# Loading fields in pairs and late weights by GpSimd's queue over 14 of 16 DMA engines

## The chip, the cores and the metric

The kernel runs on one core of one Trainium2 chip. The metric is the device time of one execution in microseconds (us). A core has five engines that matter here: TensorE (PE, with its weight loads shown apart as PEld), VectorE (DVE), ScalarE (ACT), GpSimd (POOL) and SyncE (SP, which here only issues transfers, 93 in before). Their transfers run on 16 DMA engines: the page of before books the packets of all queues on them, 99.6% of their time in sum. Times are quoted as medians. Profiled executions have a "span", which is about 1.8 us shorter than the time.

## The reference

For 1024 samples with 32 fields of 128 numbers, every pair of fields i < j (496 pairs) has its own 128 x 128 matrix:

```python
v_i = inputs[:, I_IDX, :]
v_j = inputs[:, J_IDX, :]
transformed = jnp.einsum('bpd,ped->bpe', v_i, W)
return transformed * v_j
```

The result is 496 x 128 x 1024 float32, 260 MB.

## The kernel before

The pairs run from the last field down to the first, so that fields are needed one after the other: all pairs with the same i form a *field group*. Except for the first 15 pairs, each matmul is done as three, with x and W split into high and low parts to keep accuracy. For the weights, ScalarE makes the high part (`wh` in the profiles), GpSimd the low part (`wl`) and a difference (`wd`):

```python
    def split_w(c, u):          # c is a chunk of 2 pairs
        ...
        nc.scalar.mul(h, raw, 1.0 - 2.0**-13)
        nc.gpsimd.tensor_tensor(l, raw, h.bitcast(F32), ALU.subtract)
        nc.gpsimd.tensor_scalar(d, h.bitcast(F32), EPS, 1.0, ALU.mult, ALU.mult)
        nc.gpsimd.tensor_tensor(d, l.bitcast(F32), d.bitcast(F32), ALU.subtract)
```

At each field group GpSimd also has to split the next field (`split_x`: twice `xl`, twice a scaling, and for later fields twice `xd`).

The main loop, for each half pair `u` (cut):

```python
            if u % 2 == 0 and j == i + 1 and 0 < i - 2 - XLEAD:
                load_x(i - 2 - XLEAD)          # 512 KB by SyncE, 7 field groups ahead
            first(u)                           # two matmuls, ScalarE scales the sum
            if u % 2 == 1 and q in w_at:
                load_w(w_at[q])                # 8 pairs of weights, 512 KB by SyncE
        ...
            second(u - LAG)                    # third matmul, VectorE multiplies by x_j
        while stores and stores[0][0] <= u - LAG:
            nc.scalar.dma_start(*stores.pop(0)[1:])   # 4 pairs, 2 MB, by ScalarE's queue
```

## Time and profile before

| | before |
|---|---|
| time, median of 3 | 755.34 us (755.04 to 755.51) |
| span; mean granted PE clock (1 is full speed) | 753.2 us; 0.994 |
| DMA | 310 MB in 33,038 packets, 412 GB/s |
| landing gap of a store: last engine after the middle one (the 9th of 16), median, 30 to 80 us / 140 to 440 us / 440 to 720 us | 1.5 / 4.2 to 4.6 / 4.2 to 4.7 us |

The last row comes from the trace's records of semaphores: each of the 16 engines reports its share of each store. VectorE's pauses end with the last of them: in 69 of the 72 pauses of over 0.7 us in before, it goes on 0.12 us after the 16th report of a transfer.

### The profile page before, as it was taken

The page shows a single profiled execution, that of the slowest core. Times are in us where ns is not written, and L with a number is a line of the kernel's source. Part 1 is how long each engine was busy: PE and PEld are TensorE (multiplying, and loading weights), DVE is VectorE, ACT ScalarE, POOL GpSimd, SP SyncE. Part 2 cuts the span into 40 slices and gives each one's busy share as a digit, 9 for nine tenths or more (in the row PEclk, how much of TensorE's full clock was granted, in tenths as well). Part 3 has the DMA queues.
Part 4 walks back from the last instruction along what each step waited for, and adds up shares of the span by engine and source line. Part 5 has one row for each costly group of instructions (what it writes and reads, how often), then busy time and mean ns, then how long its engine had stood idle before and what let it go on. Part 6 is the DMA issues. An engine that isn't in the chain of part 4 may idle for free.

```text
span 753.2 us, 10948 instructions
## 1 busy us (share of the span) xinstructions
PE 706.5 (94%) x2946; PEld 546.0 (72%) x2946; DVE 624.1 (83%) x1012; ACT 627.1 (83%) x1256; POOL 595.5 (79%) x863
## 2 busy tenths in 40 slices
PE   7989999999999999999999999999999999999993
PEld 3567776777777777777777778777777777777782
DVE  4989888888887878888878897988888889888894
ACT  1389888889988898888888889898989898988892
POOL 1788998888988987978879797888887879796660
PEclk9999999999999999999999999999999999999997
DMA  9999999999999999999999999999999999999997
GB/s 353 428 427 423 430 427 424 423 417 433 399 425 406 411 420 413 415 405 401 425 401 422 412 401 422 400 432 405 417 419 421 399 432 401 425 406 413 425 397 312
DMA packets 33038, 310.04 MB, mean 412 GB/s; under 512 B 3665, under 2 KB 3793, under 8 KB 17361
## 3 DMA queue, kind: packets, MB, share of 16 engines
q10 hardware_dynamic: 19584, 261.10, 82.5%
q1 hardware_dynamic: 13392, 48.24, 16.8%
q8 instruction: 24, 0.39, 0.2%
q14 instruction: 38, 0.30, 0.1%
HBM read 49.28 MB, written 260.05 MB: 411 GB/s over the span
## 4 chain that ended last, share of the span: by engine, by line
DMA 43%; PE 32%; DVE 13%; POOL 6%; ACT 2%; issue 2%; DVEq 0%; ACTq 0%; POOLq 0%
DMA out_dram<-ot 42%; PE po L172 19%; DVE ot L187 12%; PE po L181 9%; PE po L169 4%; ACT po L173 2%; POOL xd L122 2%; POOL wl L102 1%; POOL xl L117 1%; POOL wd L104 1%; ACT wh L101 1%; POOL xl L118 1%; POOL wd L103 0%; DVE xd L217 0%; DMA x<-in_xt_dram 0%
## 5 line engine op out<-in xcount | busy, mean ns | idle before, releaser
L187 DVE TENSOR_TENSOR ot<-po,x 128x512 f32<-128x512 f32 x992 | 610.1, 682 | 118.5 <-DMA out_dram<-ot 50.7
L173 ACT ACTIVATE po<-po 128x512 f32<-128x512 f32 x962 | 543.4, 583 | 94.3 <-PE po L172 41.0
L172 PE MATMUL po<-xh,wh 128*128 128x512 f32 x962 | 382.8, 398 | 21.4 <-DVE ot L187 20.5
L172 PE MATMUL po<-xl,wl 128*128 128x512 f32 x962 | 376.6, 392 | 4.8 <-POOL wl L102 4.8
L181 PE MATMUL po<-xd,wd 128*128 128x512 f32 x962 | 375.2, 390 | 4.0 <-DVE xd L217 3.4
L172 PEld LDWEIGHTS po<-xh,wh 128*128 128x128 f32 x962 | 180.4, 188 | 88.8 <-DVE ot L187 50.8
L102 POOL TENSOR_TENSOR wl<-w,wh 128x256 fp32r<-128x256 f32 x241 | 178.3, 740 | 73.3 <-ACT wh L101 71.8
L181 PEld LDWEIGHTS po<-xd,wd 128*128 128x128 f32 x962 | 180.6, 188 | 44.0 <-ACT po L173 4.7
L172 PEld LDWEIGHTS po<-xl,wl 128*128 128x128 f32 x962 | 180.7, 188 | 42.2 <-POOL wl L102 8.8
L104 POOL TENSOR_TENSOR wd<-wl,wd 128x256 fp32r<-128x256 f32 x241 | 180.5, 749 | 20.1
L103 POOL TENSOR_SCALAR wd<-wh 128x256 fp32r<-128x256 f32 x241 | 101.3, 420 | 20.3
L101 ACT ACTIVATE wh<-w 128x256 fp32r<-128x256 f32 x241 | 99.5, 413 | 5.1 <-DVE ot L187 3.3
L117 POOL TENSOR_TENSOR xl<-x,xh 128x512 fp32r<-128x512 f32 x52 | 67.2, 1292 | 18.1 <-ACT xh L116 17.7
L122 POOL TENSOR_TENSOR xd<-xh,xl 128x512 fp32r<-128x512 f32 x32 | 41.4, 1294 | 2.7
L116 ACT ACTIVATE xh<-x 128x512 fp32r<-128x512 f32 x52 | 32.5, 629 | 11.3 <-DMA x<-in_xt_dram 11.2
L118 POOL TENSOR_SCALAR xl<-xl 128x512 fp32r<-128x512 f32 x52 | 33.7, 649 | 4.6
L169 PE MATMUL po<-x,w 128*128 128x512 f32 x60 | 27.8, 623 | 4.4 <-DMA x<-in_xt_dram 4.3
L169 PEld LDWEIGHTS po<-x,w 128*128 128x128 f32 x60 | 11.6, 198 | 19.8 <-issue 12.3
L217 DVE TENSOR_TENSOR xd<-xh,xl 128x512 fp32r<-128x512 f32 x20 | 17.2, 859 | 0.0
L116 ACT ACT_TABLE_LOAD x1 | 1.3, 1283 | 2.6 <-issue 2.6
L233 POOL MEMSET const-float32-0.0<- 128x1 f32 x1 | 0.1, 98 | 0.2 <-issue 0.2
L233 POOL MEMSET const-bfloat16-1.0<- 128x1 bf16 x1 | 0.1, 101 | 0.0
(2 smaller groups left out, 0.2 us busy)
## 6 DMA issues: line engine op xcount, KB each, us to landing
out_dram<-ot ACTq DMA_DIRECT2D x122, 2048.0 KB, 12.5
w<-in_wt_dram SPq DMA_DIRECT2D x61, 512.0 KB, 10.3
x<-in_xt_dram SPq DMA_DIRECT2D x30, 512.0 KB, 16.0
out_dram<-ot ACTq DMA_DIRECT2D x6, 512.0 KB, 9.2
x<-in_xt_dram ACTq DMA_DIRECT2D x4, 256.0 KB, 5.9
out_dram<-ot ACTq DMA_DIRECT2D x4, 256.0 KB, 8.2
w<-in_wt_dram SPq DMA_DIRECT2D x1, 448.0 KB, 4.7
w<-in_wt_dram SPq DMA_DIRECT2D x1, 64.0 KB, 2.9
```

The costliest lines, as they stand in the source:

```text
L101: nc.scalar.mul(h, raw, 1.0 - 2.0**-13)
L102: nc.gpsimd.tensor_tensor(l, raw, h.bitcast(F32), ALU.subtract)
L103: nc.gpsimd.tensor_scalar(d, h.bitcast(F32), EPS, 1.0, ALU.mult, ALU.mult)
L104: nc.gpsimd.tensor_tensor(d, l.bitcast(F32), d.bitcast(F32), ALU.subtract)
L117: nc.gpsimd.tensor_tensor(l, x_sb[f][:, s], h.bitcast(F32), ALU.subtract)
L118: nc.gpsimd.tensor_scalar(l, l.bitcast(F32), 1.0 / EPS, 1.0, ALU.mult, ALU.mult)
L122: nc.gpsimd.tensor_tensor(d, h.bitcast(F32), l.bitcast(F32), ALU.subtract)
L169: nc.tensor.matmul(po[u], w_raw[q // WL][:, q % WL, :], x_sb[i][:, s], start=True, stop=True)
L172: nc.tensor.matmul(po[u], w_s[c][t][:, r], x_s[i][t][:, s], start=t == 0, stop=t == 1)
L173: nc.scalar.mul(po[u], po[u], 1.0 + EPS)
L181: nc.tensor.matmul(po[u], w_s[q // WC][2][:, r], x_s[i][2][:, s], start=False, stop=True, skip_group_check=True)
L187: nc.vector.tensor_tensor(ots[g][:, k, s], po.pop(u), x_sb[j][:, s], ALU.mult)
```

## The change

The intent is to give two of the 16 DMA engines less work, because one engine lands its share of the stores of before late (by 4.2 to 4.7 us from 140 us on). The x loads of fields 1 to 23 are joined in pairs (22 with 23, 20 with 21, and so on), and every second weight chunk from 41 on is changed too. 112 of the 128 rows go by GpSimd's queue in a shape meant for 14 engines; the other 16 rows go by SyncE, meant as one to each engine. So two engines are to get one row of such a load instead of eight. Small dummy loads ("marks") are meant to hold the position at which the loads start, so that all of them spare the same two engines, 3 and 4 as I count them from 0. Which engines the loads spare is my plan: before has no such transfer. The host reorders the rows to match. Cut to its core:

```diff
+NE = 14
+ROWS = 8 * NE
+WAPART = range(41, NQ // WL, 2)
...
+    def move_on(k):
+        nc.gpsimd.dma_start(out=mark[: 2 * k], in_=xt[: 2 * k, 0, :16].rearrange("(b a) n -> a b n", a=k))
+
+    def load_apart(dst, src):
+        nc.gpsimd.dma_start(out=dst[:ROWS], in_=src[:ROWS].rearrange("(b a) m n -> a b m n", a=NE))
+        nc.sync.dma_start(out=dst[ROWS:], in_=src[ROWS:])
+        move_on(16 - NE)
...
     def load_w(c, splits=(0, WL), eng=nc.sync):
         w_raw[c] = rpool.tile([P, WL, P], F32, tag="w", name=f"w_{c}")
+        if c in WAPART:
+            load_apart(w_raw[c], wt[c])
+            return
...
+    move_on(5)
...
-            if u % 2 == 0 and j == i + 1 and 0 < i - 2 - XLEAD:
-                load_x(i - 2 - XLEAD)
+            f = i - 2 - XLEAD
+            if u % 2 == 0 and j == i + 1 and f > 0 and f % 2 == 1:
+                load_x_apart(max(f - 1, 1), min(f, 2))
...
-    nc = _bacc.Bacc("TRN2", target_bir_lowering=False, num_devices=1, dynamic_dma_scratch_size=256)
+    nc = _bacc.Bacc("TRN2", target_bir_lowering=False, num_devices=1, dynamic_dma_scratch_size=2048)
```

The last line raises `dynamic_dma_scratch_size` from 256 to 2048; it is called the reserve (for GpSimd's descriptors) below.

More of the change, by code (lines that the diff above doesn't have):

```diff
@@ L87, with load_x_apart @@
     w_raw = {}
+    mark = xpool.tile([32, 16], F32, tag="mark", name="mark")
+    def move_on(k):
[4 more added lines that the diff above has]
+        move_on(16 - NE)
+    def load_x_apart(f, n):
+        t = xpool.tile([P, n, BT], F32, tag=f"x{f}", name=f"x_{f}")
+        load_apart(t, xt[:, f : f + n, :])
+        for k in range(n):
+            x_sb[f + k] = t[:, k, :]
     def load_w(c, splits=(0, WL), eng=nc.sync):
         w_raw[c] = rpool.tile([P, WL, P], F32, tag="w", name=f"w_{c}")
+        if c in WAPART:
+            load_apart(w_raw[c], wt[c])
+            return
         for a, b in zip(splits, splits[1:]):
@@ L217 @@
             nc.vector.tensor_tensor(*later.pop(0)[1:], ALU.subtract)
+    move_on(11)
     assert not todo and not later and not stores
@@ L230 @@
     xt = _np.ascontiguousarray(x.transpose(2, 1, 0))
+    later = xt[:ROWS, 1 : NF - 3 - XLEAD].reshape(NE, 8, -1, BT)
+    xt[:ROWS, 1 : NF - 3 - XLEAD] = later.transpose(1, 0, 2, 3).reshape(ROWS, -1, BT).copy()
     wt = _np.ascontiguousarray(w[perm].reshape(NQ // WL, WL, P, P).transpose(0, 3, 1, 2))
-    nc = _bacc.Bacc("TRN2", target_bir_lowering=False, num_devices=1, dynamic_dma_scratch_size=256)
+    for c in WAPART:
+        wt[c, :ROWS] = wt[c, :ROWS].reshape(NE, 8, WL, P).transpose(1, 0, 2, 3).reshape(ROWS, WL, P).copy()
+    nc = _bacc.Bacc("TRN2", target_bir_lowering=False, num_devices=1, dynamic_dma_scratch_size=2048)
     arrays, args = {}, []
```

## The prediction

> **What bounds the kernel now.** I read the busy shares first, then the queues, the waits, the stretches of the timeline, and last the raw landing times of single transfers.
>
> ```profile
> PE 706.5 (94%) x2946; PEld 546.0 (72%) x2946; DVE 624.1 (83%) x1012; ACT 627.1 (83%) x1256; POOL 595.5 (79%) x863
> ...
> DMA packets 33038, 310.04 MB, mean 412 GB/s; under 512 B 3665, under 2 KB 3793, under 8 KB 17361
> ## 3 DMA queue, kind: packets, MB, share of 16 engines
> q10 hardware_dynamic: 19584, 261.10, 82.5%
> q1 hardware_dynamic: 13392, 48.24, 16.8%
> q8 instruction: 24, 0.39, 0.2%
> q14 instruction: 38, 0.30, 0.1%
> ```
>
> The page of before: no compute engine is full (PE's 94% is modelled and overlaps itself), but the four queues' packets add up to 99.6% of the time of 16 DMA engines. The kernel is bound by DMA, and 261 of its 310 MB are the result itself. These bytes can't be saved; only their spread over the engines can change.
>
> ```profile
> core 0: us, PE busy (x) PEld busy (x) DVE busy (x) ACT busy (x) POOL busy (x), PEclk, DMA share, GB/s
> 20.00:140.00 120.00, 112.10 (x450) 82.73 (x449) 105.03 (x167) 93.44 (x192) 104.13 (x143) 1.00 1.01 427
> 140.00:440.00 300.00, 284.22 (x1204) 222.33 (x1203) 247.21 (x406) 260.62 (x523) 253.00 (x363) 1.00 1.01 414
> 440.00:720.00 280.00, 273.47 (x1175) 217.63 (x1174) 240.05 (x393) 250.52 (x501) 223.75 (x336) 1.00 1.00 413
> ```
>
> Three stretches of before; the last column is GB/s. The DMA share is full in all three, yet the rate falls from 427 to 414 GB/s. [...]so "full" hides something. The semaphore increments of each store tell what: 16 engines report each store separately. At 43 us the last of them comes 1.8 us after the first; the gap grows to about 5 us by 140 us and stays there. From 560 us on, typically 13 engines land within 0.5 us of each other, one 1 to 2 us later, and **one engine 4.5 to 5.4 us later**. An output tile is free only when all 16 have landed, so that engine sets the pace[...]:
>
> ```profile
> engine line waited for: us in total, times, longest us
> POOL wl L102 <- ACT wh L101: 71.8, 99, 2.8
> PEld po L172 <- DVE ot L187: 50.8, 79, 1.2
> DVE ot L187 <- DMA out_dram<-ot: 50.7, 58, 1.8
> ```
>
> The waits of before: VectorE waits 50.7 us for stores to free its tile. What slows the one engine is very probably q8: 24 packets of 16 KB, about one each 30 us, with a mean of some 0.95 us, against 0.611 us for a 16 KB packet of a store. That is 24 x 0.95 = 22.8 us, the right size, and the landing gap grows by about 1 us at each.
>
> [...]
>
> **The change part by part.** The host reorders rows so that 112 of 128 have an outer dimension of 14[...]. The other 16 rows go by SyncE[...]. [...] This concerns 11 loads of two fields (rows of 8 KB), 1 of one field and 11 weight chunks (rows of 4 KB); the order listing shows these 23 loads and 25 marks new on POOL, compute unchanged.
>
> *The two spared engines.* A 4 KB packet takes 0.159 us in the trace. For an 8 KB row I take 0.309 us, what most of q14's 8 KB packets took. Per engine 7 rows less: 11 x 7 x 0.309 = 23.8, plus 12 x 7 x 0.159 = 13.4, in all 37 us. That exceeds the 22.8 us of q8, so the slow engine, if it is spared, stops being last. In time it fits too: about 24 us are removed by 330 us, when 10 fetches (9.5 us) have happened; the weight chunks, from about 480 us on, take off 1.1 us per 23 us against 0.7 us of fetches.
>
> *The other fourteen.* One row more per load: 11 x 0.309 + 12 x 0.159 = 5.3 us each; joining two 4 KB packets to one 8 KB saves 11 x 8 x (0.318 - 0.309) = 0.8. Net +4.5 us. They now set the pace, and the small fetches of the other engines (q14, 43 x 0.309 = 13 us in all, 3 us if one engine has a quarter) come to light: +2.
>
> *The sum for DMA.* Bound before: common work + 22.8. Bound after: common work + 4.5 + 2. Gain 16.3 us, if compute can follow.
>
> *Compute.* At the end of before, with no weights left to load, stores are issued every (737.88 - 710.86)/5 = 5.40 us: compute's own pace there. Between 498 and 596 us they come every 97.0/17 = 5.71 us. The slow engine's work per store is 8 x 0.611 + 4 x 0.159 + 0.95 x 5.7/30 = 5.70 us, which agrees; a fast one's is 5.52, plus 0.04 after the change. That leaves 0.1 to 0.2 us between DMA and compute, so hiccups of compute will cost something that the waiting store queue hides today: I take 2 us off.
>
> *POOL.* 48 more issues; no trace here has one. [...] Mostly hidden. But [...]laid against before's POOL timeline, the loads leave some 5 us later than SyncE's did. Nine of the 11 weight chunks still have 13 to 18 us before their first use; chunk 55 has 8.4 and chunk 57 only 6.0, while landing took a median of 10.3 us: some 1 to 2 us of stall. At the start, the pair 22/23 now leaves at once and shares the engines with the first fields that PE waits for: 112 x 8 KB at 427 GB/s is 2.1 us, of which perhaps 1 delays the end, as those bytes have to move anyway.
>
> Sum: 755.3 - 16.3 + 2 + 1.5 + 1 = 743.5; the landing gap before the last store (2.8 us between the last two engines' and the rest's end) is in the 16.3 already. As the slow engine may have cost a little more than its fetches (the fall from 427 to 414 GB/s over 580 us would be worth 18 us), I set 742.5.
>
> **The rivals.** [...]the slow engine isn't 3 or 4. Then the slow engine gets 5 us more work: about 758. Against it: a held position with an odd constant like 5 looks like a measured one. I give it a tenth. *GpSimd's issue is dear* (3 us or more each): POOL is at 85 to 88% before 240 us, its splits get late, and PE waits for wl; the gain is eaten, about 750 to 756. For it: POOL is waited for 8.8 + 4.8 us already. Against it: POOL itself waits 71.8 us for ScalarE, so it has room. *Compute becomes the bound sooner*: at 5.6 us per store in the late part only 0.1 x 54 stores = 5 us are won there, for 746. *Everything is balanced perfectly*: 310 MB at 427 GB/s is 726 us, plus 2.5 us of start and 2 of tail, and 2.2 between span and time: 733.
>
> **Range and chances.** The centre lies 1.7% below before; faster by over 2% means below 740.2, which needs compute to follow almost free. That is a third. Slower by over 2% would need the wrong engines and a dear POOL together.
>
> **What would show it.** Right: the gap between the last engine's landing of a store and the middle one falls from 5 us to 1 to 2; GB/s between 140 and 720 us rises to about 420; VectorE's wait for stores shrinks; store intervals near 500 to 600 us are about 5.6. Wrong: the gap stays at 5 us or grows (wrong engines); waits for POOL's wl grow beyond some 25 us (issue is dear); PE first starts 3 us later (the early pair). A DMA landing that ScalarE's wh waits for near chunk 57 shows the late issue.

## More of the kernel before

The weight splits are asked for three chunks ahead, in four buffers:

```python
    wpool = ctx.enter_context(tc.tile_pool(name="ws", bufs=4))
    ...
        todo.append(((c - 3) * WC + 1, max(c * WC, nq0), lambda u, c=c: split_w(c, u)))
```

The prediction shows the queues, the stretches and the largest waits. Two more waits of before are needed later. They are lines of the view of waits: engine, tile and line that waited, what it waited for; us in total, times, longest.

```profile
PEld po L172 <- POOL wl L102: 8.8, 10, 1.2
PE po L172 <- POOL wl L102: 4.8, 10, 0.8
```

PE and its weight loads seldom wait for GpSimd's low part of the weights.

The start of before, in stretches of the timeline (span of the stretch, its length, then busy us and number of instructions of PE, PEld, DVE, ACT and POOL, granted PE clock, DMA share, GB/s):

```profile
5.00:10.00 5.00, 4.93 (x9) 1.56 (x8) 0.69 (x1) 0.00 (x0) 0.00 (x0) 1.00 1.03 411
10.00:15.00 5.00, 5.00 (x13) 2.24 (x12) 4.46 (x8) 0.00 (x0) 0.00 (x0) 1.00 1.03 410
20.00:30.00 10.00, 10.00 (x25) 4.50 (x24) 9.64 (x15) 0.72 (x2) 9.25 (x12) 1.00 1.06 435
20.00:70.00 50.00, 46.36 (x175) 32.21 (x174) 44.92 (x70) 32.57 (x68) 40.93 (x57) 1.00 1.02 427
```

PE is busy from the first fields on, and DMA moves 410 to 435 GB/s.

## The result

| | before | after |
|---|---|---|
| time, median (lowest to highest) | 755.23 (755.04 to 755.51), 5 runs | 762.70 (762.33 to 764.58), 5 runs |
| ratio after / before | | 1.0106, 95% interval 1.0092 to 1.0120 |
| span; mean granted PE clock | 753.2; 0.994 | 760.9; 0.981 |
| store landing gap, 30 to 80 / 140 to 440 / 440 to 720 us | 1.5 / 4.2 to 4.6 / 4.2 to 4.7 | 1.9 / 1.4 to 1.9 / 1.1 to 1.8 us |
| first store issued; the 11th; the last | 15.2; 61.7; 745.0 us | 21.9; 72.5; 754.6 us |

All runs were counted as fast: they lie within 0.3% of the fastest of their kernel. A ratio here is always the mean time of one kernel's fast runs over the mean of the other's fast runs of the same rounds, so it is not quite the ratio of the medians. The kernel became 1% slower. The prediction's centre was 742.5 us, a gain of 1.7%; 762.70 is 20.2 us above it, on the other side of before.

The page of after, its busy times and its queues (packets, MB, share of 16 engines):

```profile
PE 703.5 (92%) x2946; PEld 555.5 (73%) x2946; DVE 664.4 (87%) x1012; ACT 625.2 (82%) x1256; POOL 623.3 (82%) x911
...
q10 hardware_dynamic: 19584, 261.10, 82.0%
q1 hardware_dynamic: 9232, 32.64, 11.7%
q0 software_dynamic: 4112, 15.61, 5.9%
```

GpSimd's new queue, q0, carries 15.6 MB that SyncE's q1 carried before. It takes 5.9% for them, more per byte than q1 took before (0.38% per MB against 16.8/48.24 = 0.35%). The three stretches that the prediction shows of before:

```profile
20.00:140.00 120.00, 108.61 (x419) 78.71 (x418) 105.26 (x161) 85.53 (x174) 102.58 (x140) 0.99 1.00 396
140.00:440.00 300.00, 285.21 (x1223) 229.96 (x1222) 267.15 (x413) 263.35 (x532) 264.36 (x383) 0.99 1.01 420
440.00:720.00 280.00, 267.83 (x1162) 217.88 (x1161) 255.87 (x388) 247.47 (x497) 236.37 (x355) 0.99 1.00 410
```

Only the middle stretch improved: 420 GB/s instead of 414. The first one lost (396 instead of 427; 419 matmuls instead of 450), and the last one lost (410 instead of 413). The waits of after:

```profile
POOL wl L131 <- ACT wh L130: 44.9, 72, 3.3
DVE ot L217 <- DMA out_dram<-ot: 35.6, 30, 3.4
PEld po L202 <- POOL wl L131: 33.9, 23, 2.7
PE po L202 <- POOL wl L131: 25.2, 19, 2.3
ACT wh L130 <- DMA w<-in_wt_dram: 4.2, 2, 2.5
```

VectorE waits less for stores, as intended (35.6 us against 50.7). GpSimd itself waits less (44.9 against 71.8), which says that it is fuller. PE now waits for GpSimd: 25.2 + 33.9 us against 4.8 + 8.8. (The two overlap: at the stop at 195 us below, the weight load waits 2.4 us and PE 2.0 us.) And ScalarE waits twice for a weight chunk that came late; before had no such wait. The start:

```profile
5.00:10.00 5.00, 3.41 (x4) 0.52 (x3) 0.00 (x0) 0.00 (x0) 0.55 (x1) 1.00 1.08 301
10.00:15.00 5.00, 2.26 (x3) 1.17 (x4) 0.69 (x1) 0.00 (x0) 0.00 (x0) 0.67 0.99 232
20.00:70.00 50.00, 44.30 (x151) 27.82 (x150) 40.46 (x63) 26.04 (x54) 38.51 (x52) 1.00 1.01 383
```

This is a reading to remember: the DMA share is 1.08 and 0.99, so all engines are "busy", yet they move 301 and 232 GB/s instead of 411 and 410. Busy time is time in which packets are under way; here the packets themselves were slow. Between 4 and 16 us an 8 KB packet of GpSimd's queue took a median of 584 ns; from 70 us on it took 309 ns.

PE started 0.2 us later than before, not the 3 us that the prediction named as a sign; its stop came after the first matmuls (4.3 us, until 12.7 us). It also ran at half speed (granted clock 0.5) for 6.8 us from 11.7 us on. That is not what made the first store late: f5 below, in its one run, has no such stretch there, and its first store comes at 22.3 us.

Laid store by store against before, after is 6.7 us behind at the first store, 10.8 at the 11th, and 13.1 at the 21st. It then wins back slowly to 6.0 us behind at 624 us, is 11.5 us behind again at 670 us and 9.6 at the last store, and its tail after that is 1.9 us shorter. So there are a loss in the first 70 us, a modest gain in the middle, and a loss near the end. In the middle, most store intervals are now exactly PE's own pace: 24 matmuls at 0.2265 us are 5.44 us. Between 240 and 440 us, 68% of the intervals are below 5.5 us (before: 21%), but the mean only falls from 6.00 to 5.81 us, because once per field group PE stands still. One such place, single instructions of PE (start, us, engine, line, operation; in brackets the idle time and what ended it):

```profile
195.14 0.50 PE L202 MATMUL po<-xl,wl 128*128 128x512 f32 x1 [1.98 <-POOL wl L131]
...
196.27 0.63 PE L211 MATMUL po<-xd,wd 128*128 128x512 f32 x1
...
199.81 0.40 PE L211 MATMUL po<-xd,wd 128*128 128x512 f32 x1
```

PE waits 1.98 us for GpSimd's low weights, and from 196.3 to 199.4 us its matmuls come at half the pace (0.43 us apart instead of 0.23): after the gap the granted clock was 0.5 for 3.4 us. The stretch of the timeline says so, in its third number from the end:

```profile
196.00:199.40 3.40, 3.40 (x10) 2.63 (x9) 2.20 (x4) 1.75 (x4) 3.15 (x6) 0.50 1.00 425
```

Besides the start, this happens four times in after, at 121, 196, 353 and 677 us, and not once in before until its end.

### The profile page after: what moved, and what is told of

Read it like the earlier page. It is cut to its first block, busy times and chain, and to the rows that moved or that the text cites.

```text
span 760.9 us, 11038 instructions
## 1 busy us (share of the span) xinstructions
PE 703.5 (92%) x2946; PEld 555.5 (73%) x2946; DVE 664.4 (87%) x1012; ACT 625.2 (82%) x1256; POOL 623.3 (82%) x911
## 3 DMA queue, kind: packets, MB, share of 16 engines
q1 hardware_dynamic: 9232, 32.64, 11.7%
## 4 chain that ended last, share of the span: by engine, by line
PE 71%; DMA 12%; POOL 11%; DVE 3%; issue 2%; ACT 0%; DVEq 0%; SPq 0%; POOLq 0%; ACTq 0%
PE po L202 46%; PE po L211 23%; DMA out_dram<-ot 8%; POOL xd L151 3%; DMA w<-in_wt_dram 3%; POOL wl L131 3%; DVE ot L217 2%; POOL xl L146 2%; PE po L199 2%; DMA x<-in_xt_dram 1%; POOL wd L133 1%; POOL xl L147 1%; POOL wd L132 1%; DVE xd L248 1%; ACT po L203 0%
## 5 line engine op out<-in xcount | busy, mean ns | idle before, releaser
L217 DVE TENSOR_TENSOR ot<-po,x 128x512 f32<-128x512 f32 x992 | 649.5, 687 | 87.7 <-DMA out_dram<-ot 35.6
L202 PE MATMUL po<-xl,wl 128*128 128x512 f32 x962 | 379.8, 395 | 25.5 <-POOL wl L131 25.2
L202 PE MATMUL po<-xh,wh 128*128 128x512 f32 x962 | 378.6, 394 | 7.5 <-DVE ot L217 7.3
L202 PEld LDWEIGHTS po<-xl,wl 128*128 128x128 f32 x962 | 181.9, 189 | 71.6 <-POOL wl L131 33.9
L131 POOL TENSOR_TENSOR wl<-w,wh 128x256 fp32r<-128x256 f32 x241 | 179.9, 747 | 49.1 <-ACT wh L130 44.9
L202 PEld LDWEIGHTS po<-xh,wh 128*128 128x128 f32 x962 | 182.2, 189 | 50.7 <-DVE ot L217 12.4
L199 PE MATMUL po<-x,w 128*128 128x512 f32 x60 | 31.0, 681 | 8.9 <-DMA x<-in_xt_dram 8.9
L199 PEld LDWEIGHTS po<-x,w 128*128 128x128 f32 x60 | 12.6, 217 | 26.4 <-issue 19.2
L101 POOL DMA_DIRECT2D mark<-in_xt_dram x25 | 14.1, 565 | 7.4 <-DMA mark<-in_xt_dram 4.2
L248 DVE TENSOR_TENSOR xd<-xh,xl 128x512 fp32r<-128x512 f32 x20 | 17.7, 884 | 0.1
L104 POOL DMA_DIRECT2D x<-in_xt_dram x12 | 7.7, 638 | 0.1
L104 POOL DMA_DIRECT2D w<-in_wt_dram x11 | 7.1, 643 | 0.0
## 6 DMA issues: line engine op xcount, KB each, us to landing
out_dram<-ot ACTq DMA_DIRECT2D x122, 2048.0 KB, 10.7
w<-in_wt_dram SPq DMA_DIRECT2D x50, 512.0 KB, 10.3
w<-in_wt_dram POOLq DMA_DIRECT2D x11, 448.0 KB, 10.8
```

Source lines behind the costliest of these rows:

```text
L199: nc.tensor.matmul(po[u], w_raw[q // WL][:, q % WL, :], x_sb[i][:, s], start=True, stop=True)
L202: nc.tensor.matmul(po[u], w_s[c][t][:, r], x_s[i][t][:, s], start=t == 0, stop=t == 1)
L217: nc.vector.tensor_tensor(ots[g][:, k, s], po.pop(u), x_sb[j][:, s], ALU.mult)
```

## The experiments

The theories after reading the two traces were these. **A**, the start: loads over 14 engines in the first 70 us are slow and come when nothing is won by sparing two engines. **B**, GpSimd: 48 more issues and DMA-free stretches make it late at field groups. **C**, the late chunks 55 and 57 stall ScalarE. The rival to all three was that the balance itself did not work. The experiments come in the order of the argument; letters are those of the calls. Unless a number of runs is given, a time is the median of 2 to 5 runs. Before, run beside them, had medians of 755.03 to 755.23.

### Does the position of the engines matter?

**e4**: the position at which the loads are to start is one lower.

```diff
-    move_on(5)
+    move_on(4)
```

> The changed kernel with the held position one lower (first mark over 4 engines, last over 12): engines 2 and 3 are spared instead of 3 and 4. Theory (one slow engine, position known): if engine 3 is the slow one, landing gaps and time stay as in the changed kernel (gap about 2 us, 762 to 764); if it is engine 4, the gap of the last engine is 5 us or more again between 200 and 700 us and the time is 765 to 775. Rival (the position on the ring does not matter, or two engines are slow): neither, or a gap in between.

Measured: 775.33 us, ratio 1.0266, 12.6 us more than after. The landing gap went back to 3.1 to 4.6 us between 140 and 540 us (after: 1.4 to 1.9 between 140 and 440). So the position matters: the one in the changed kernel is right, and the rival falls. If the loads spare the engines that the plan names, the late one is the engine that after spares and this version does not, 4 in my count; no trace names it.

### The start

**e1**: only the first pair, fields 22 and 23, is loaded singly by SyncE as before.

```diff
-            if u % 2 == 0 and j == i + 1 and f > 0 and f % 2 == 1:
+            if u % 2 == 0 and j == i + 1 and f >= 22:
+                load_x(f)
+            elif u % 2 == 0 and j == i + 1 and f > 0 and f % 2 == 1:
```

> The changed kernel with one thing undone: fields 22 and 23 are loaded as before, one by one by SyncE in their old places; all later pairs and weights stay on GpSimd's queue. Theory (the early pair costs the start): the first store is issued at about 15 to 16 us instead of 21.9, PE's 4.3 us wait near 12.7 us is gone, and the time falls by about 7 us, to 755 to 756, so level with before; the rest of the loss at the start (3 us more by the fifth store, from the second pair) stays. Rival (the start is late for another reason, such as the marks or the order on SyncE, or the start does not matter as bytes have to move anyway): first store still after 19 us, or time still at 761 to 763.

Measured: 758.67 us, ratio 1.0044, so 4.0 us less than after (the theory expected about 7). The first store is issued at 15.3 us as in before, but the 11th is still 6.6 us late. The next pairs do damage too, as the stretch from 20 us shows:

```profile
20.00:30.00 10.00, 10.00 (x24) 4.37 (x23) 10.00 (x15) 0.72 (x2) 8.56 (x10) 1.00 1.05 361
30.00:40.00 10.00, 8.67 (x33) 5.68 (x31) 6.19 (x11) 6.11 (x13) 8.20 (x14) 1.00 1.00 409
40.00:50.00 10.00, 6.92 (x27) 5.39 (x28) 6.07 (x11) 5.55 (x11) 7.15 (x11) 0.92 1.01 419
```

Again full DMA shares, but 361 GB/s instead of the 435 of before in the first ten us. Later, PE and VectorE do less, because they wait for stores that queue behind (VectorE 10.7 us between 20 and 75 us, against 1.6 in before). The landings add a second cause: at the fifth store two engines are done 4.8 to 5.0 us before the middle one. In before the last engine is only 1.5 us late at that time (median of 30 to 80 us). The two engines were relieved before there was anything to relieve them of.

Why are the packets slow? **e3** sends the same loads by GpSimd's queue, but in the plain form: 128 rows, 16 engines, no marks, host order as in before.

```diff
     def load_apart(dst, src):
-        nc.gpsimd.dma_start(out=dst[:ROWS], in_=src[:ROWS].rearrange("(b a) m n -> a b m n", a=NE))
-        nc.sync.dma_start(out=dst[ROWS:], in_=src[ROWS:])
-        move_on(16 - NE)
+        nc.gpsimd.dma_start(out=dst, in_=src)
```

> The same loads leave by GpSimd's queue, but as whole 128-row transfers over all 16 engines, without marks and without the 16 rows by SyncE. Nothing is rebalanced. Theory (the 14-engine layout is what makes these loads slow[...]): the 8 KB packets of GpSimd's queue in the first 15 us take about 0.31 us instead of 0.6, GB/s between 5 and 15 us is near 400 instead of 232 to 301, and the first store is issued at 17 to 18 us. The landing gap of the slow engine stays at 5 us, time 755 to 760. Rival (GpSimd's queue is slow as such): packets stay at 0.6 us and the first store stays at 21 to 22 us.

Measured: 759.52 us, ratio 1.0056. Its first store is issued at 17.7 us, as the theory said: 4.2 us earlier than in after, and 2.5 us later than in before. From 395 to 664 us its stores are within 1.8 us of before's, and only then does it fall behind, by 6.4 us at 682 us, where ScalarE waits for two late weight chunks (7.0 us). So early pairs on the same queue, over 16 engines, cost little that lasts. Whether the 2.5 us come from the pairing or from GpSimd's queue was not tested.

**f5** keeps the 14-engine form, but reads its rows in plain order from a copy in memory, so that only the writing side is as in after (one look, state unknown).

> The changed kernel, with the fields' 112 rows read from a copy in blocks of 9 rows[...]; where they are written stays the same. Theory[...]: 8 KB packets of GpSimd's queue between 8 and 14 us still take about 0.6 us, GB/s between 10 and 15 us stays near 230, first store at 21 to 22 us. Rival (the order of reading in HBM is what slows them): packets at 0.31 us and the first store at 17 to 18 us, as in the run over 16 engines.

Measured: 761.84 us, in one run. The stretch from 5 to 10 us, first of e3, then of f5:

```profile
5.00:10.00 5.00, 2.81 (x4) 0.50 (x2) 0.00 (x0) 0.00 (x0) 0.00 (x0) 1.00 1.02 416
```

```profile
5.00:10.00 5.00, 3.35 (x4) 0.50 (x2) 0.00 (x0) 0.00 (x0) 0.55 (x1) 1.00 1.08 288
```

In the plain form the same queue moves 416 GB/s, its 8 KB packets at a median of 309 ns. In the 14-engine form it moves 288 GB/s with packets of 606 ns, even when the read order is plain. So GpSimd's queue as such is not slow, and the read order is not the reason. Of what e3 dropped, the 16 rows by SyncE left only at 16.3 us, after the slow stretch. What is left, besides the small marks, is the 14-engine form on the side where it is written. Why its packets take twice the time (606 ns here, 584 in after, against 309) is not shown. In after, from 70 us on, with stores under way, the median is back at 309 ns.

### GpSimd and the field groups

**e2**: only the weight chunks go apart, all x loads as in before.

```diff
-                load_x_apart(max(f - 1, 1), min(f, 2))
+                load_x(f)
```

> Only the 11 late weight chunks go apart; all fields are loaded as before by SyncE. Theory (balance is worth little because POOL's splits and PE are nearly the bound themselves): stores up to 480 us come as in the kernel before, within 1 us; after that the last engine's landing gap falls from 5 us towards 2, and the time is 752 to 756, a gain of at most 3 us. Rival (DMA balance pays in full in the late part): 54 stores times 0.12 us is 6 us less, plus 2 us at the end: 747 to 748.

Measured: 756.72 us, ratio 1.0019 (0.9998 to 1.0039). Until 482 us it runs with before (within 0.6 us from 60 us on). Then the landing gap falls from 4.8 to between 1.2 and 1.9 us, but nothing is won: PE and PEld now wait 10.7 + 15.5 us for wl, and the stores end 3.1 us later, most of it from one such stop near 510 us and from the late chunks near 670 us. So balance in the last third won nothing here; the run does not separate the waits for wl from the late chunks 55 and 57. (k2 below, without these two, shows that the other nine win 1.6 us once the late x loads go apart too.)

**h1** asks how fast compute is by itself. It stores only half of each tile of four pairs. Its output is wrong, which doesn't matter for the time.

```diff
-            stores.append((u + SLAG, out[g], ots[g]))
+            stores.append((u + SLAG, out[g, :, : OG // 2], ots[g][:, : OG // 2]))
```

> Wrong result on purpose: the kernel before, but each 2 MB store writes only the first two of its four pairs, so DMA has about 40% less to move and compute is left as it was. It measures compute alone. Theory (compute is held at each field group by 1 to 2 us, in which PE waits for the splits, and that pace is nearly DMA's of before): PE's floor of 481 pairs of 6 matmuls of 0.2265 us is 654 us, plus 32 at the start and 8 at the end, plus 25 groups of some 1.4 us, makes 725 to 742. Rival (compute keeps the 5.40 us a store that the prediction took, so DMA alone holds the kernel before): 693 to 708.

Measured: 729.04 us, ratio 0.9656. **h3** does the same with weight splits one chunk further ahead.

```diff
-    wpool = ctx.enter_context(tc.tile_pool(name="ws", bufs=4))
+    wpool = ctx.enter_context(tc.tile_pool(name="ws", bufs=5))
...
-        todo.append(((c - 3) * WC + 1, max(c * WC, nq0), lambda u, c=c: split_w(c, u)))
+        todo.append(((c - 4) * WC + 1, max(c * WC, nq0), lambda u, c=c: split_w(c, u)))
```

> Wrong result on purpose, as in the run with half stores, but the weight splits run one chunk (two pairs) further ahead, with five instead of four buffers of them. Theory (PE's gap at each field group is POOL falling behind while it splits the field, and a deeper lead absorbs it): the gaps on POOL's wl go and the time falls by at least 15 us against the half stores alone. Rival (the gaps come from VectorE or ScalarE, or POOL is short of time over the whole group): within 5 us of it.

Measured: 708.99 us, ratio 0.9391. The waits of h1, then of h3:

```profile
PEld po L172 <- POOL wl L102: 30.9, 21, 2.3
PE po L172 <- POOL wl L102: 22.1, 21, 1.8
```

```profile
PEld po L172 <- POOL wl L102: 10.9, 11, 1.8
PE po L172 <- POOL wl L102: 6.4, 9, 1.4
```

With DMA out of the way (in h1, VectorE waits 0.4 us in all for stores), the compute of before takes 729 us, and it has the waits for wl that after has (22.1 + 30.9 us): they are in the kernel already, hidden behind the stores. A deeper lead takes 20 us off, and PE then runs at its pace of 5.44 us per store nearly all the time (between 440 and 640 us, every interval is below 5.5 us). So the field-group stops come from GpSimd falling behind while it splits a field, and a lead of three chunks does not cover it.

**f1**, **f2**, **f4** move all of GpSimd's `xd` work to VectorE: f1 in before as a control, f2 in after, f4 in after without the first pair and with chunks 55 and 57 by SyncE.

```diff
-SHARED = 10
+SHARED = 26
```

> Control: the kernel before, with the last subtraction of the field split (xd) on VectorE for all fields instead of the first ten, so that 32 instructions of 1.3 us leave POOL. Theory (before is held by its slow DMA engine, POOL only nearly so): time unchanged within 3 us, 752 to 757, POOL's busy time down by 41 us. Rival (POOL was the bound of before as well): 745 or less. Other rival (VectorE has no room): 760 or more.

> The changed kernel with the same relief of POOL (all xd on VectorE). Theory (once DMA is balanced, POOL's splits at the start of each field group hold PE, and POOL's 48 new issues of 0.6 us come on top): PE's matmul and weight-load waits for POOL's wl, 59 us together, fall under 30 us, and the time falls by 4 to 8 us to 754 to 758; the 6.7 us at the start stay. Rival (POOL is not what holds it; the loss is all at the start and in DMA): 760 to 763.

> All three suspected costs removed at once: no early pair, all xd on VectorE, and weight chunks 55 and 57 (whose lead was too short) loaded by SyncE. Theory (costs add): 758.7 of the run without the early pair, less 4 to 8 for POOL and 2 for the chunks, is 749 to 753, so some 4 us faster than before. Rival (PE's own pace and the slow 14-engine loads hold it): 755 to 758.

Measured: f1 755.40 (ratio 1.0003), f2 766.16 (1.0149), f4 760.23 (1.007; its four runs lie between 756.9 and 765.4). f1 agrees that before is held by its stores. The idea that relieving GpSimd in this way would cure after fell. In f2, PE and PEld wait for VectorE instead:

```profile
PEld po L202 <- DVE ot L217: 39.5, 45, 3.5
PE po L202 <- DVE ot L217: 21.2, 26, 3.0
```

So the hiccup seems to move from GpSimd to VectorE. Not all of f2's loss is this: ScalarE also waits longer for the two late chunks (9.7 us, against 4.2 in after). f4 has no early pair and no late chunks, and is still no faster than e1 (758.67), which has both chunks.

### The deeper lead with loads apart

**g1** is before with the deeper lead (a control). **g3** is after with it, without the first pair, and with 55 and 57 by SyncE; the reserve goes down from 2048 to 768 with it (at 2048 the program with five buffers does not build: 46.78 KB per partition are left for the output tiles, which take 48).

> Control: the kernel before with the weight splits one chunk further ahead. Theory (its slow DMA engine holds it, the store queue hides PE's gaps at field groups): 753 to 757, unchanged. Rival (the field groups held before too): 745 to 750.

> The changed kernel without the early pair, with chunks 55 and 57 by SyncE, and with the weight splits one chunk further ahead (five buffers; GpSimd's descriptor space 768 instead of 2048 bytes to make room). Theory (the DMA balance was real, but its gain fell to PE's waits at the field groups): those waits nearly go, DMA is the bound again at its better pace, and the time is 744 to 751, faster than before by 0.5 to 1.5%. Rival (POOL is short of time over the whole, or the slow 14-engine loads hold it): 755 to 759 as in the run without the early pair.

Measured: g1 756.39 us (20 runs, ratio 1.002), g3 755.06 us (19 runs from 747.63 to 762.15, four of them counted slow; ratio 0.999, of the fast ones). g1 says that before is not held by GpSimd. g3 was a miss: PE's waits for wl were nearly gone (0.9 + 1.3 us), but nothing was won. Its profile shows the early x loads (11th store 6.9 us late) and four waits of ScalarE for weight chunks (10.2 us together).

### Only the late x loads

**j1** keeps only the x loads of fields 15 and below apart, from about 70 us on. No weights go apart, and the lead is the old one.

```diff
-WAPART = range(41, NQ // WL, 2)
+WAPART = ()
...
+            if u % 2 == 0 and j == i + 1 and f >= 16:
+                load_x(f)
+            elif u % 2 == 0 and j == i + 1 and f > 0 and f % 2 == 1:
```

> Only the x loads of fields 15 and below go apart (eight loads of two fields or one, from about 70 us on); fields 16 to 22 are loaded singly by SyncE, no weights go apart, weight splits as in before. Theory 1 (the late x loads balance the engines at no cost of their own; the 14-engine loads hurt only in the first 70 us): the slow engine is relieved of 7 x (7 x 0.309 + 0.159) = 16 us, the landing gap in the middle falls from 4.6 to under 2.5 us, stores 4 to 20 are as early as in before (within 1 us); but PE still waits for GpSimd's wl at the field groups, so only part is won: 749 to 755 us. Rival (GpSimd loads cost in POOL and in half-speed packets what balance gains, wherever they are): 755 to 760 us.

Measured: 750.09 us (749.46 to 752.05), ratio 0.9939 (0.9927 to 0.9951). This is the first version that beats before. The landing gap between 140 and 440 us is 1.8 to 2.3 us, the early stores are within 0.1 us of before until 50 us and at most some 2.4 us later up to 120 us, and 2.6 to 4 us earlier from 400 us on. So the later eight of the loads win by themselves, and the rival that GpSimd's loads cost what they give wherever they are falls.

**j2** is j1 with the deeper lead (reserve 768). **j3** is j2 with nine weight chunks apart (41 to 53, 59, 61) and all weight loads asked for two pairs earlier.

> The run before plus weight splits one chunk further ahead (five buffers), as in the run g3 but without apart loads in the first 70 us and without late weight chunks. Theory 1: PE's waits for GpSimd's wl go (under 10 us), no waits of ScalarE's wh for a weight load over 1 us, the start is as in before, and the engines' balance is worth something at last: 742 to 750 us, a version that beats both. Rival (GpSimd's loads cost what balance gains): within 1% of before, 750 to 760 us, with the loss in some new wait of PE or VectorE.

> The run before plus nine weight chunks apart (41 to 53, 59, 61), and every weight load asked for two pairs earlier, to match the deeper splits. Theory 1: another 9 x 7 x 0.159 = 10 us off the slow engine, which keeps the gap under 2 us in the last third as well: 739 to 749 us, 0 to 5 us below the run without. Rival (late weight loads and GpSimd's extra issues cost more than they give): 3 to 10 us above the run without, with waits of ScalarE's wh for weight loads or of PE for GpSimd's wl between 480 and 720 us.

Measured: j2 757.76 us (13 runs, 753.0 to 760.7, ratio 1.0026), j3 754.49 us (22 runs, 748.9 to 758.2, ratio 0.9991). Both missed. In j2, PE no longer waits for wl, but VectorE waits more for stores than in j1. The wait in j1, then in j2:

```profile
DVE ot L217 <- DMA out_dram<-ot: 43.9, 40, 3.7
```

```profile
DVE ot L217 <- DMA out_dram<-ot: 61.1, 49, 3.4
```

From 340 us on, two or three engines of j2 are 2 to 5 us behind the middle one, not only one. **k1** tests whether the smaller reserve does this: j1 with the reserve of 768 and nothing else.

```diff
-    nc = _bacc.Bacc("TRN2", target_bir_lowering=False, num_devices=1, dynamic_dma_scratch_size=2048)
+    nc = _bacc.Bacc("TRN2", target_bir_lowering=False, num_devices=1, dynamic_dma_scratch_size=768)
```

> The run j1 with the reserve for GpSimd's descriptors cut from 2048 to 768, nothing else. The three runs with the deeper weight lead and apart loads (g3, j2, j3) all had to cut it so, and all three spread over 8 to 15 us, while every run with 2048, and the deeper lead without apart loads, stayed within 1 to 4 us. Theory 1 (the small reserve, or the addresses that it shifts, makes the spread and the second and third late engine): median 752 to 758, a spread of over 4 us, and from 340 us on a second engine more than 2.5 us behind the middle one. Theory 2 (the deeper lead with apart loads does it): as j1, 749 to 752 us, spread under 3 us, second engine 1.2 to 1.6 us behind.

Measured: 750.32 us (748.84 to 750.54), ratio 0.9935, as j1. So the small reserve alone costs no time. It is not quite cleared as a cause of late engines: k1's second engine is 2.1 us behind the middle one between 540 and 640 us and 3.1 between 640 and 720 (j1: 1.5 and 1.6). Nor does the wide spread belong to the deeper lead with loads apart, as my text for k1 assumed: f4 (8.5 us) and l1 below (9.5 us) have the old lead and a reserve of 2048. What makes more engines late and the times so uneven stays open.

### The best version, and the price of two chunks

**k2** is j1 with the nine weight chunks apart, asked for when before asks for them, with the old lead.

```diff
-WAPART = ()
+WAPART = (41, 43, 45, 47, 49, 51, 53, 59, 61)
```

> The run j1 plus nine weight chunks apart (41 to 53, 59, 61), asked for when before asks for them; reserve 2048, splits as in before. Theory 1 (late balance is worth something where the weights arrive in time): the gap of the last engine after 440 us falls from 3.4 to 4.2 us to under 2, and the time is 745 to 750 us. Theory 2 (as in e2, weights apart fill the queue of GpSimd at the field groups and give back what they win): the gap falls likewise, but PE's waits for GpSimd's wl grow by 5 us or more and the time is 749 to 754 us.

Measured: 748.54 us (4 runs, 747.82 to 749.46), ratio 0.9913 (0.9899 to 0.9926). This beats both kernels: 0.9% below before and 14.2 us below after. Its three stretches and the two waits:

```profile
20.00:140.00 120.00, 112.06 (x448) 83.78 (x447) 106.31 (x168) 91.72 (x189) 105.53 (x147) 0.99 1.01 419
140.00:440.00 300.00, 284.28 (x1224) 227.27 (x1223) 254.52 (x413) 263.36 (x534) 264.26 (x381) 1.00 1.01 421
440.00:720.00 280.00, 271.94 (x1179) 221.13 (x1178) 253.72 (x393) 251.38 (x504) 232.90 (x352) 0.99 1.00 414
```

```profile
PEld po L202 <- POOL wl L131: 23.7, 16, 2.5
PE po L202 <- POOL wl L131: 17.2, 14, 2.1
```

The first stretch is back at 448 matmuls and 419 GB/s, the middle is as good as in after, and the last no longer loses. PE's waits for wl are still there, but did not grow against j1 (25.8 and 17.7 us). So theory 1 held, though the gap fell under 2 us only from 540 us on (3.3 us between 440 and 540).

**l1** is k2 with all eleven chunks apart, 55 and 57 too. It is the changed kernel with only the x loads of the first 70 us undone.

> The changed kernel with one thing undone: the fields 16 to 23, which are loaded in the first 70 us, go singly by SyncE as in before; all eleven weight chunks and the x loads of fields 15 and below stay apart. It differs from the run k2 only in the chunks 55 and 57, which before asks for late. Theory 1 (the early 14-engine loads are the cost; 55 and 57 a small one): 749 to 752 us, 1 to 3 us above k2, with ScalarE's wh waiting 2 to 6 us for two weight loads. Rival (late chunks are a main cost): 753 us or more.

Measured: 753.26 us (22 runs, 750.2 to 759.7), ratio 0.9982 (0.9967 to 0.9997). My theory expected 749 to 752, the rival 753 or more: the two late chunks cost 4.7 us, more than I thought, and they make the times uneven. In the profiled run of 756.4 us:

```profile
ACT wh L130 <- DMA w<-in_wt_dram: 7.5, 2, 5.0
```

One of these waits is 5.0 us long. PE stands still for 3.95 us at 683 us, and its granted clock then is 0.5 for 6.8 us.

### The sum of the parts

The medians, all against a before of 755.0 to 755.2, make a ladder:

| step | time | difference |
|---|---|---|
| before | 755.1 | |
| + x loads of fields 15 and below apart (j1) | 750.1 | -5.0 |
| + nine weight chunks apart (k2) | 748.5 | -1.6 |
| + chunks 55 and 57 apart (l1) | 753.3 | +4.7 |
| + x loads of fields 16 to 23 apart (after) | 762.7 | +9.4 |

## Why the prediction was wrong

**The late engine** was right. "One engine 4.5 to 5.4 us later" set the pace of before, and the changed loads spare it: the gap fell to 1.1 to 1.9 us, VectorE's wait for stores from 50.7 to 35.6 us, and e4 shows that the position matters. That the fetches on q8 make it late stays an inference: the sum fits, but no run shows which engine carries them, and of q8 and q14 the page says no more than that their kind is "instruction". (Three readings were slightly off: 0.95 us is the median of q8's packets, and their mean of 0.99 gives 23.8 us; six of q14's 43 packets of 8 KB came before the span; and the gap does not grow in steps at q8's packets, but by some 0.25 us from each store to the next: from 1.33 us at 72 us to 2.55 at 103 us, with no packet of q8 from 73 to 105 us.) 140 to 440 us came to the 420 GB/s that were named; 440 to 720 us did not (410).

**"Compute"** failed, and with it the sum for DMA. It took compute's pace as 5.40 us per store, from the end of the run, where GpSimd has no weights left to load and few splits to make. It left out the stop of 1 to 2 us in each field group. "I take 2 us off" stood for this. h1 measured compute alone at 729 us, where a pace of 5.40 would have given 693 to 708, and in it 22.1 us of PE's waits for wl. DMA and compute are nearly even, so each hides the other's hiccups, and removing one bound brings out the other. Of the 16.3 us predicted for DMA, the runs gave 6.6 us (j1 and k2 together, with 17 of the 23 loads apart). The fourth sign named, store intervals of about 5.6 us near 500 to 600 us, did not come: the mean between 440 and 640 us is 5.74 us, against 5.69 in before.

**"POOL ... Mostly hidden"** looked at an average. An issue is cheap: 0.56 us for a mark, 0.64 for an x load (medians). The marks:

```profile
L101 POOL DMA_DIRECT2D mark<-in_xt_dram x25: 549/558/692, 1.4 to 744.3; - x25
```

(Minimum, median and maximum in ns.) But the 21% of before in which GpSimd is not busy are no room at the moment of need. At a field group GpSimd splits a field, and PE needs the next weights before it has caught up (in after PE waits 1.98 us for them at 195 us). The rival "GpSimd's issue is dear" named the right wait (waits for wl beyond 25 us would show it; they were 25.2 and 33.9), but gave its own reason for it. How much the issues add is not shown: h1 has nearly the same waits (22.1 and 30.9) without any. What the prediction missed is that these waits were in the kernel already.

**Chunks 55 and 57** were named with 8.4 and 6.0 us before their first use, against 10.3 us of landing. The stall is there, but it was sized at "1 to 2 us" for 4.7 measured (l1 against k2): in l1's profile a late chunk stops ScalarE for 5.0 us, then PE for 3.95 us, and PE's granted clock is then 0.5 for 6.8 us.

**The start** was the largest error: where the prediction had "of which perhaps 1 delays the end", the early pairs cost 9.4 us (after against l1). I counted bytes at 427 GB/s for the pair 22/23 alone. The runs showed packets of twice the time in the first 16 us (584 ns), and three further pairs before 70 us: undoing the first pair gave 4.0 us (e1 against after), undoing the other three 5.4 (l1 against e1). And the two engines that are spared so early are done early (4.8 to 5.0 us before the middle one in e1), as the late engine was only 1.5 us late then. How the cost divides between the slow packets and the two engines that are done early is not shown; e3, which has neither, lost little that lasted. In the prediction's own working, "about 24 us are removed by 330 us, when 10 fetches (9.5 us) have happened" says that relief comes before the burden; I took it as a comfort, and it is a cost.

**The clock** was not in the prediction at all. Four times in after a gap of PE of 1.8 to 2.3 us was followed by 3.4 us at half speed (granted clock 0.5). Gaps of 1.9 and 2.3 us at 244 and 518 us were not, so the length of a gap alone does not tell. At half speed 3.4 us of work are lost by half, so an estimate from these durations is 4 x 1.7 = 7 us of PE's time, of which DMA hides a part.

What stays open: why the deeper weight lead, worth 20 us without DMA's limit (h3), is lost again together with loads apart (g3, j2, j3), and why their times spread over 8 to 15 us, as those of f4 and l1 do (8.5 and 9.5).

## What to carry to other kernels

When a slow DMA engine holds a kernel, find out what compute alone takes (store half) before counting the gain: here it was 729 of 755 us, and its hiccups took most of the room. Put such relief where the lag has built up, and only on loads with time to spare: 17 of the 23 loads changed the time by -6.6 us, the other six (four pairs in the first 70 us, two late chunks) by +14.1 us. Here a full DMA share with fewer GB/s (1.08 at 301 GB/s) went with slow packets (584 ns for 8 KB, against 309); compare the ns per packet before thinking of bytes.
